# Where the scan of a state-space layer finds its input: PSUM bank or state tile

## The chip, the cores and the metric

The kernel runs on one core of a Trainium2 chip. The metric is the device time of one execution in microseconds. A core has five engines that work side by side, each with its own queue in order: PE (TensorE, matmuls), DVE (VectorE), ACT (ScalarE), POOL (GpSimd) and SP (SyncE, which here issues the DMAs). SBUF is the large on-chip memory, PSUM the small one that PE writes, in eight banks of 128 partitions by 512 floats. POOL works on SBUF only in this kernel.

## What is computed

Four images (4, 192, 56, 56) in float32 go through four layers: a local attention with an MLP, a frequency gating, an overlapping-window attention with a gated MLP, and a selective scan over the pixels in four directions. Only the last layer matters here. For each direction it computes, with 192 channels d and 4 states n per channel:

```python
def step(h, inp):
    dt_t, u_t, B_t, C_t = inp
    dA = jnp.exp(dt_t[..., None] * A)
    h = dA * h + dt_t[..., None] * B_t[:, :, None, :] * u_t[..., None]
    y = jnp.einsum('bkdn,bkn->bkd', h, C_t)
    return (h, y)
```

## The kernel before

The layer works in chunks of 448 pixels, seven to an image. A step `t` is one chunk of one image in one direction (4 images x 4 directions x 7 chunks = 112 steps). The 192 x 4 = 768 pairs of channel and state make six groups of 128 partitions; a half `h` (96 channels) is three of them. So there are 224 units `(t, h)` and 672 groups. For a unit, `scan(t, h)` does this:

- DVE multiplies `dt` by `u` into `du` (L2371 where the direction runs along rows, L2374 along columns, there with a strided `u`): 96 partitions, both inputs in SBUF.
- PE spreads each 32 channels of `du` over 128 partitions with a 0/1 matrix (L2381), into three PSUM banks.
- DVE multiplies each bank by B (`b_`, a tile in SBUF, called `bc` in the profile), in place in the bank (L2387). This is the product of dt u and B.
- DVE scans (L2403): `state = da * state + product` along the 448 pixels, `da` from SBUF, the product from the bank, the result into a state tile `st` in SBUF. The first value is a column of the state tile that the chunk before left.
- POOL multiplies the state tile by C (`c_`, also `bc` in the profile) into `da` (L2410): both inputs in SBUF.
- PE sums the four states of each channel (L2426), and DVE adds the sums into `y` (L2431, L2436 or L2440).

The decays `da` are made in `decay(t, h)`: a DMA spreads `dt` (L2348) and ACT takes the exponential (L2356). `load(t)` brings B, C and the low-rank dt from DRAM, `sizes` makes `dt` on PE (L2310) and ACT (L2322). Beside the scans run the front of the next image (`begin`: a layer norm L2079 to L2100, projections L2134, a depthwise convolution on PE L2167, ACT L2184, `product` L2218) and the end of the last one (`final`: a layer norm, a gate on POOL L2245, the output projection L2254, a sum on DVE L2265). Of the layer before, L1569 is a DVE multiply-add in its convolution, and L1430 a square on POOL.

The order of the instructions on every engine is fixed when the kernel is built. Each activity is a generator that yields, ahead of each piece of work, the engine, a cost, and the buffers that it takes; `Order.run` always starts the piece that can start first by these costs, with a small preference by place. `take` and `done` hand out and return buffers: `bank` is the pool of the eight PSUM banks, shared by everything that PE computes; `st` is 12 state tiles, `da` 10, `du` 3. A state tile is returned once the next chunk's scan has read its last column. The semaphores between the engines are put in by the tile framework from what is read and written.

Of the kernel before, what the change touches and what calls it, by code (L numbers as in the profile page):

```python
# [17 lines left out]
ALU = mybir.AluOpType  # L18
# [24 lines left out]
NS, DTR, SCH = 4, 12, 448  # L43
# [222 lines left out]
def rows2(ap, w=W):  # L266
    return ap.rearrange("p (y x) -> p y x", x=w)


class Order:  # L270
# [29 lines left out]
    def take(self, kind="bank"):  # L300
        slot = min((s for s in self.kinds[kind] if s[0] is not None), key=lambda s: s[0])
        slot[0] = None
        return slot[1]

    def done(self, tile):

        (slot,) = (s for slots in self.kinds.values() for s in slots if s[1] is tile)
        slot[0] = self.end + self.LATENCY
# [57 lines left out]
def on_pe(n, *takes, ready=None):  # L366

    return "PE", 0.0019 * n, takes, None, ready
# [6 lines left out]
def on_dve(*n, takes=(), ready=None, each=0.00105):  # L375
    return "DVE", sum(0.08 + each * i for i in n), takes, None, ready


def on_scan(n, ready):
    return "DVE", 0.1 + 0.0023 * n, ("st",), None, ready  # L380


def on_act(*n, takes=(), table=None, ready=None):
# [3 lines left out]
def on_pool(*n, each=0.0011, takes=()):  # L387
    return "POOL", sum(0.2 + each * i for i in n), takes, None, None
# [1601 lines left out]
def layer3(tc, order, pools, src, packs, aps, dst):  # L1990
# [7 lines left out]
    nc = tc.nc  # L1998
    take, done = order.take, order.done
# [71 lines left out]
    def gone(*what):  # L2071
        return what in passed
# [258 lines left out]
    def use(t, h):  # L2331

        users[t, h] = users.get((t, h), 0) + 1
        if users[t, h] == 2:
            done(sized[t][0][h])
# [23 lines left out]
    def scan(t, h):  # L2359

        b, o, s, c = steps[t]
        head = c == (NSC - 1 if s else 0)
        last = c == (0 if s else NSC - 1)
        px = slice(c * SCH, (c + 1) * SCH)
        yield lambda: t in sized and (2 * t + h == 0 or gone("multiplied", 2 * t + h - 1))
        dts, b_, c_ = sized[t]
        u = us[b % 2]
        yield on_dve(SCH, takes=("du",), each=0.0018 if o else 0.0015)
        du = take("du")
        if o == 0:  # L2370
            nc.vector.tensor_mul(du, dts[h], u[:HALF, h, px])  # L2371
        else:
            uv = u[:HALF, h].rearrange("p (y x) -> p x y", x=W)[:, 8 * c : 8 * c + 8]
            nc.vector.tensor_mul(rows2(du, H), rows2(dts[h], H), uv)  # L2374
        use(t, h)

        yield on_pe(500, *["bank"] * 3)
        tiles = [take() for _ in range(3)]
        for j in range(3):
            r = slice(32 * j, 32 * j + 32)  # L2380
            nc.tensor.matmul(tiles[j][:, :SCH], w["c96.rep"][r], du[r], start=True, stop=True)  # L2381
        done(du)
        passed.add(("multiplied", 2 * t + h))
        ends = []
        for j in range(3):
            yield on_dve(SCH, ready=order.end if j else None)
            nc.vector.tensor_mul(tiles[j][:, :SCH], tiles[j][:, :SCH], b_)  # L2387
            ends.append(order.end + order.LATENCY)
        if h == 1:
            done(b_)  # L2390
        das, sts = [], []
        for j in range(3):
            g = 3 * h + j
            yield lambda: (t, h, j) in decays and (head or (t - 1, g) in states)
            da, at = decays.pop((t, h, j))
            yield on_scan(SCH, ready=max(at, ends[j]))
            sts.append(take("st"))
            r = slice(None, None, -1 if s else 1)
            first = 0.0
            if not head:  # L2400
                before = states.pop((t - 1, g))
                first = before[:, 0:1] if s else before[:, SCH - 1 : SCH]
            nc.vector.tensor_tensor_scan(  # L2403
                sts[j][:, r], da[:, r], tiles[j][:, :SCH][:, r], first, ALU.mult, ALU.add
            )
            done(tiles[j])
            if not head:
                done(before)
            yield on_pool(SCH, each=0.0024)
            nc.gpsimd.tensor_mul(da, sts[j], c_)  # L2410
            das.append(da)
            if last:
                done(sts[j])
            else:
                states[t, g] = sts[j]
        if h == 1:
            done(c_)
            del sized[t]

        yield lambda: b == 0 or gone("read", b - 1, c if (o, s) == (0, 0) else 0)  # L2420
        yield lambda: (o, s) == (0, 0) or len(started) == 2 * NSC * (b + 1)
        yield lambda: s == 0 or o == 1 or added[b] >= 6 * NSC + 2 * (NSC - 1 - c) + h
        yield on_pe(600, "bank")
        py = take()
        for j in range(3):
            nc.tensor.matmul(py[32 * j : 32 * j + 32, :SCH], w["c128.sum"], das[j], start=True, stop=True)  # L2426
            done(das[j])
        yield on_dve(SCH)
        sums = py[:HALF, :SCH]
        if (o, s) == (0, 0):  # L2430
            nc.vector.scalar_tensor_tensor(  # L2431
                y[:HALF, h, px], u[:HALF, h, px], d_sum[:, h : h + 1], sums, ALU.mult, ALU.add
            )
            started.add((t, h))
        elif o == 0:
            nc.vector.tensor_add(y[:HALF, h, px], y[:HALF, h, px], sums)  # L2436
        else:

            yv = y[:HALF, h].rearrange("p (y x) -> p y x", x=W)[:, :, 8 * c : 8 * c + 8]
            nc.vector.tensor_add(yv, yv, sums.rearrange("p (x y) -> p y x", y=H))  # L2440
        done(py)
        added[b] += 1
        if o == 0 and s == 1 and h == 1:
            passed.add(("summed", b, c))
        if added[b] == 8 * NSC:
            passed.add(("scanned", b))
# [6 lines left out]
    n = 8 * NSC  # L2453
# [5 lines left out]
    for t in range(len(steps)):  # L2459
        add(2 * t - 5, load(t))  # L2460
        if t % 2 == 0:
            add(2 * t - 3, sizes((t, t + 1)))
        for h in range(2):
            add(2 * t + h - 1, decay(t, h))
            add(2 * t + h, scan(t, h))
# [5 lines left out]
    def keep_late(*args):  # L2471
        return keep(*args, pool=late)
# [7 lines left out]
        da=keep_late("da", [SCH], 10),  # L2480
        st=keep_late("st", [SCH], 12),
# [43 lines left out]
```

## Time and profile before

| | |
|---|---|
| median of 3 runs | 5724.87 us (5719.17 to 5725.76) |
| profiled execution | 5731.28 us, span 5729.5 us |
| mean granted TensorE clock | 0.929 |
| busy, whole span | PE 4866.4 us (85%), DVE 4140.6 (72%), ACT 2655.4 (46%), POOL 1699.9 (30%) |
| scans (L2403) | 672, from about 3990 to 5702 us |
| products (L2387) | 672, 415 us of DVE, 618 ns each |

In the lines of the profile an instruction is named by its line in the kernel, its engine, its operation and its tiles (`out<-in`), then shapes and count; a group's line ends with busy time, mean ns of one, and the engine's idle time before it with what ended it. `bank` is a PSUM bank; every other tile named here is in SBUF. In a timeline line the first number is the start and the second the time, in us. A line of one source line's instructions gives count, least, median and longest duration in ns, first and last start.

### The profile page before, as it was taken

Reading aid. Unit: us, or ns where it says so; the run is one execution under the profiler, and the core shown is the slowest. Engines: PE = TensorE matmul, PEld = TensorE weight load, DVE = VectorE, ACT = ScalarE, POOL = GpSimd, SP = SyncE. Lnnn points to the kernel's source line nnn. Section 1 sums busy time; section 2 is a strip of 40 time slices with the busy share of each in tenths; the row PEclk is TensorE's granted clock in tenths of the full one; section 3 lists DMA queues with packets and bytes.
Section 4 is the critical chain, followed back from the end, with each engine's and each line's share of the span. In section 5 each row is a group of like instructions: output and inputs, shape, how many; then the busy total and the mean of one; then the engine's idle time right before and its main releaser. Section 6 shows DMA issues by size and latency. Waiting matters only on the chain. (4 is left out here: it accounts for less than half of the span.)

```text
span 5729.5 us, 137267 instructions
## 1 busy us (share of the span) xinstructions
PE 4866.4 (85%) x58114; PEld 2407.0 (42%) x58114; DVE 4140.6 (72%) x6600; ACT 2655.4 (46%) x4271; POOL 1699.9 (30%) x1688
## 2 busy tenths in 40 slices
PE   4988998998899687898898888868888888888777
PEld 2444554454454444555555555534332232222112
DVE  5788447544744026888988888883678999998997
ACT  0122323212232215555555555546776776676544
POOL 0000000000000013433333433321345555555564
PEclk9999998999999798999999999989998999999998
DMA  6132224333332521000000000002456656566654
GB/s 185 53 80 60 66 60 105 64 88 91 76 69 56 99 77 37 14 22 21 17 22 18 19 20 21 16 26 60 122 135 157 160 145 172 155 149 167 165 149 109
DMA packets 356373, 475.97 MB, mean 83 GB/s; under 512 B 43600, under 2 KB 354256, under 8 KB 355248
## 3 DMA queue, kind: packets, MB, share of 16 engines
q1 hardware_dynamic: 355760, 467.20, 32.9%
q8 instruction: 458, 7.50, 0.5%
q14 instruction: 155, 1.27, 0.1%
HBM read 249.73 MB, written 63.17 MB: 55 GB/s over the span
## 5 line engine op out<-in xcount | busy, mean ns | idle before, releaser
L2410 POOL TENSOR_TENSOR da<-st,bc 128x448 f32<-128x448 f32 x672 | 857.0, 1281 | 751.5 <-DVE st L2403 600.1
L731 PE MATMUL bank<-X,wu 64*49 64x392 f32 x6720 | 610.5, 509 | 89.2 <-DVE X L710 85.9
L2403 DVE TENSOR_TENSOR_SCAN st<-da,st,bank 128x448 f32<-128x448 f32 x576 | 646.3, 1133 | 4.3 <-POOL da L2410 1.8
L838 POOL TENSOR_TENSOR attn<-attn,rs 112x1568 f32<-112x1568 f32 (+1 forms) x24 | 67.1, 2795 | 1726.5 <-DVE rs L836 989.9
L2356 ACT ACTIVATE da<-da,a_neg 128x448 f32<-128x448 f32 x672 | 410.1, 659 | 161.9 <-DMA da<-dt 150.2
L357 ACT ACT_TABLE_LOAD x373 | 478.6, 1283 | 6.6
L2387 DVE TENSOR_TENSOR bank<-bank,bc 128x448 f32<-128x448 f32 x672 | 382.9, 618 | 83.4 <-PE bank L2381 78.2
L731 PEld LDWEIGHTS bank<-X,wu 64*49 64x49 f32 x6720 | 247.6, 123 | 416.1 <-issue 366.4
L2426 PE MATMUL bank<-da,w_c 128*32 128x448 f32 x1344 | 348.8, 575 | 85.3 <-POOL da L2410 66.3
L2381 PE MATMUL bank<-du,w_c 32*128 32x448 f32 x1344 | 291.1, 643 | 105.2 <-DVE du L2371 59.2
L1569 DVE SCALAR_TENSOR_TENSOR bxn<-bapad,w_b,bxn 96x448 f32<-96x448 f32 (+2 forms) x448 | 318.7, 756 | 0.0
L1026 ACT ACTIVATE hm<-bank,w_a 128x448 f32<-128x448 f32 x168 | 106.3, 633 | 435.6 <-PE bank L1017 428.2
L1032 PE MATMUL bank<-hm,w_a 128*96 128x448 f32 x672 | 285.1, 555 | 16.7 <-ACT hm L1026 16.6
L1017 PE MATMUL bank<-xc,w_a 128*128 128x448 f32 x672 | 283.4, 551 | 0.6 <-DVE xc L998 0.6
L1430 POOL TENSOR_TENSOR bsq<-bsq 128x448 f32<-128x448 f32 (+7 forms) x120 | 144.5, 1206 | 446.9 <-ACT bsq L1427 401.8
L678 ACT ACTIVATE q<-bank,qk_bias,qk_scale 128x280 f32<-128x280 f32 (+2 forms) x216 | 116.9, 544 | 294.4 <-PE bank L664 251.2
L2134 PE MATMUL bank<-row,w_c 128*96 128x448 f32 x448 | 206.5, 599 | 29.7 <-DVE row L2100 27.9
L1488 PE MATMUL bank<-bxn,w_b 128*96 128x336 f32 (+2 forms) x576 | 214.3, 498 | 19.0 <-DVE bxn L1440 16.7
L754 ACT COPY sm<-bank 128x392 f32<-128x392 f32 x96 | 43.0, 489 | 380.6 <-PE bank L731 368.2
L2381 PEld LDWEIGHTS bank<-du,w_c 32*128 32x128 f32 x1344 | 92.1, 199 | 299.7 <-DVE du L2371 76.0
L998 DVE SCALAR_TENSOR_TENSOR xc<-bank,w_a,xc 96x224 f32<-96x224 f32 x112 | 44.9, 441 | 226.3 <-PE bank L988 124.5
L1763 PE MATMUL bank<-bzpad,b_diag 32*32 32x224 f32 (+2 forms) x8064 | 182.7, 371 | 24.1 <-ACT bzpad L1735 12.7
(333 smaller groups left out, 10015.4 us busy)
## 6 DMA issues: line engine op xcount, KB each, us to landing
da<-dt SPq DMA_DIRECT2D x672, 224.0 KB
vb<-vmem SPq DMA_DIRECT2D x576, 98.0 KB
bc<-prod SPq DMA_DIRECT2D x224, 224.0 KB
xq<-x SPq DMA_DIRECT2D x132, 210.0 KB
xc<-x SPq DMA_DIRECT2D x56, 336.0 KB
row<-x SPq DMA_DIRECT2D x56, 336.0 KB
xs<-x SPq DMA_DIRECT2D x28, 336.0 KB
vmem<-vt SPq DMA_DIRECT2D x56, 168.0 KB
```

What stands on the lines that cost most here:

```text
L357: self.nc.scalar.preload_act_table_set(table)
L731: nc.tensor.matmul(pm[a][outs[i], : WIN * W].rearrange("p (y x) -> p y x", x=W), wu[halves[a], k, dx], xt[halves[a], :, i, dx : dx + W], s ...
L1017: nc.tensor.matmul(ph[:, :CH], w["a128.c1T"][:, k, 128 * m : 128 * m + 128], xt[:, k], start=(k == 0), stop=(k == 1),)
L1032: nc.tensor.matmul(acc[h][:HALF, :CH], w["a128.c2T"][:, m, HALF * h : HALF * h + HALF], hm, start=(m == 0), stop=(m == 5),)
L1488: nc.tensor.matmul(rows2(pq[:HALF, :m]), w["b128." + wn][:, k, HALF * h : HALF * h + HALF], out[:, k], start=(k == 0), stop=(k == 1),)
L1569: nc.vector.scalar_tensor_tensor(dst, x, wt[:, t : t + 1], dst, ALU.mult, ALU.add)
L2356: nc.scalar.activation(da, da, AF.Exp, scale=a_neg[:, k, g : g + 1])
L2381: nc.tensor.matmul(tiles[j][:, :SCH], w["c96.rep"][r], du[r], start=True, stop=True)
L2387: nc.vector.tensor_mul(tiles[j][:, :SCH], tiles[j][:, :SCH], b_)
L2403: nc.vector.tensor_tensor_scan(sts[j][:, r], da[:, r], tiles[j][:, :SCH][:, r], first, ALU.mult, ALU.add)
L2410: nc.gpsimd.tensor_mul(da, sts[j], c_)
L2426: nc.tensor.matmul(py[32 * j : 32 * j + 32, :SCH], w["c128.sum"], das[j], start=True, stop=True)
```

## The change

The state tile is taken at the product instead of at the scan. The product writes it and returns the bank at once; the scan reads the product from the state tile and writes its result over it.

```diff
 def on_scan(n, ready):
-    return "DVE", 0.1 + 0.0023 * n, ("st",), None, ready
+    return "DVE", 0.1 + 0.0023 * n, (), None, ready
...
-        ends = []
+        ends, sts = [], []
         for j in range(3):
-            yield on_dve(SCH, ready=order.end if j else None)
-            nc.vector.tensor_mul(tiles[j][:, :SCH], tiles[j][:, :SCH], b_)
+            yield on_dve(SCH, takes=("st",), ready=order.end if j else None)
+            sts.append(take("st"))
+            nc.vector.tensor_mul(sts[j], tiles[j][:, :SCH], b_)
+            done(tiles[j])
             ends.append(order.end + order.LATENCY)
...
-        das, sts = [], []
+        das = []
...
             yield on_scan(SCH, ready=max(at, ends[j]))
-            sts.append(take("st"))
...
             nc.vector.tensor_tensor_scan(
-                sts[j][:, r], da[:, r], tiles[j][:, :SCH][:, r], first, ALU.mult, ALU.add
+                sts[j][:, r], da[:, r], sts[j][:, r], first, ALU.mult, ALU.add
             )
-            done(tiles[j])
```

Since the order on every engine is worked out from these costs and buffers, the order of the last layer's instructions can change with it.

## The prediction

> **What bounds the kernel now.** I read the page first: it gives one profiled execution of 5731.28 us (span 5729.5), 6.4 us above the median of 5724.87; the working below is made against 5731 and 6 us are taken off at the end. The change touches only the scans of the last layer, which run from 3980 to 5705 us, so the second view is the busy time by stretch, for the middle of that stage:
>
> ```profile
> core 0: us, PE busy (x) PEld busy (x) DVE busy (x) ACT busy (x) POOL busy (x), PEclk, DMA share, GB/s
> 4300.00:5650.00 1350.00, 1106.23 (x6709) 336.56 (x6710) 1237.75 (x1603) 872.92 (x1342) 764.33 (x610) 0.92 0.61 157
> ```
>
> DVE is busy 92% there (1237.75 of 1350) and idle for 112 us; over the whole stage (the same view for 3980 to 5705) it is busy 1507.69 of 1725, idle 217. POOL is busy 57%. So DVE sets the pace: time added to its queue moves the end, unless it fills one of these 217 us. Third, the page's groups:
>
> ```profile
> L2410 POOL TENSOR_TENSOR da<-st,bc 128x448 f32<-128x448 f32 x672 | 857.0, 1281 | 751.5 <-DVE st L2403 600.1
> L2403 DVE TENSOR_TENSOR_SCAN st<-da,st,bank 128x448 f32<-128x448 f32 x576 | 646.3, 1133 | 4.3 <-POOL da L2410 1.8
> L2387 DVE TENSOR_TENSOR bank<-bank,bc 128x448 f32<-128x448 f32 x672 | 382.9, 618 | 83.4 <-PE bank L2381 78.2
> ```
>
> Each scan (L2403) is followed by a POOL multiplication of its result (L2410). Fourth, what single lines took, least, median and most:
>
> ```profile
> L2371 DVE TENSOR_TENSOR du<-dt,u x112: 590/596/2593, 3980.6 to 5685.8; 96x448 f32<-96x448 f32 x112
> L2374 DVE TENSOR_TENSOR du<-dt,u x112: 946/970/1012, 4134.5 to 5574.9; 96x448 f32<-96x448 f32 x112
> L2440 DVE TENSOR_TENSOR y<-y,bank x112: 581/607/631, 4152.8 to 5589.6; 96x448 f32<-96x448 f32 x112
> L2403 DVE TENSOR_TENSOR_SCAN st<-da,st,bank x576: 1108/1135/1156, 4010.9 to 5700.4; 128x448 f32<-128x448 f32 x192
> L2410 POOL TENSOR_TENSOR da<-st,bc x672: 1119/1134/1852, 3990.8 to 5702.5; 128x448 f32<-128x448 f32 x168
> ```
>
> L2440 and L2403, with one large input in SBUF and one in PSUM, never stretch. L2371, with both large inputs in SBUF, stretches from 596 to 2593 ns, and POOL's L2410 from 1134 to 1852. The timeline shows why, at two places:
>
> ```profile
> 4356.17 1.13 POOL L2410 TENSOR_TENSOR da<-st,bc 128x448 f32<-128x448 f32 x1 [3.79 <-DVE st L2403]
> 4356.46 1.32 DVE L2371 TENSOR_TENSOR du<-dt,u 96x448 f32<-96x448 f32 x1
> ...
> 4621.39 0.97 DVE L2374 TENSOR_TENSOR du<-dt,u 96x448 f32<-96x448 f32 x1
> 4621.62 1.75 POOL L2410 TENSOR_TENSOR da<-st,bc 128x448 f32<-128x448 f32 x1 [1.50 <-DVE st L2403]
> 4622.27 1.15 DVE L2403 TENSOR_TENSOR_SCAN st<-da,st,bank 128x448 f32<-128x448 f32 x1
> ```
>
> At 4356 POOL is first (ends 4357.30); du, begun at 4356.46, ends 0.48 after that, at 4357.78. At 4621 du is first (ends 4622.36); POOL, begun inside it, ends 1.01 after that. The two exclude each other, whole instruction against whole instruction. The scan at 4622.27 lies over the same POOL instruction and takes its usual 1.15: today's scan is outside the exclusion. Its state column from SBUF (the first value) does not count; only its second large input in PSUM keeps it out. In the timeline 467 of the 672 scans lie beside POOL multiplications that read SBUF, 361 us in all.
>
> **The change, part by part.** (1) The product L2387 writes SBUF instead of PSUM. Nearest row: L2440, SBUF and PSUM in, SBUF out, 607 against 618 ns: -11 ns. It still reads one large input from SBUF, so like L2440 it stays out of the exclusion. (2) The scan reads its second input from SBUF: 607 against 596 (L2440 against L2371 undisturbed), again -11 ns. In place costs nothing: L2387 runs in place today. 672 x 22 ns = -15 us; bounds 0 and 672 x 2 x (618 - 594) = -32.
>
> (3) Banks come free one scan earlier. In the waits of the stage, PE waits for scans through banks 107 us in all (the largest: the weight loads of L2381 30.9, of L2310 25.0), but DVE feels PE only where it waits itself: 78.2 us for L2381, and those matmuls wait mostly for du. Bounds 0 and -78; I take -20. The Trainium skill, PSUM — Partial Sum Buffer, in its rules for kernel authors, advises to empty PSUM promptly because it is tight, which speaks for the change; had it the whole 107 us, the sum below would fall by another 87, to some +77.
>
> (4) A state tile is taken at the product, not at the scan. There are 12, 6 carry the last chunk's states, so 6 products may run ahead of their scans, two units of three; today three of 8 banks are held per unit, so at most two as well. The tile to be written was read by a POOL multiplication a chunk of work ago. I take 0 of a new wait, with the du and sums queued behind it as what it would hold up if the cover were gone.
>
> (5) The scan now has two large inputs in SBUF, da and st. No scan in this trace has that; the rows that do (L2371, L2374, and L1569 in the layer before) are all excluded with POOL, so I take it that the scan will be too; bounds: not at all, or always. The Trainium skill, SBUF — State Buffer, Who interferes with whom, says so for any DVE instruction with two SBUF inputs against a GpSimd instruction that reads SBUF, and speaks against this change; by the one row that is a scan, today's, the term below would be 0.
>
> Prices of (5). POOL behind DVE ends 0.99 after it (L2371: begins 0.16 into it, lasts 1.43, and 0.16 + 1.43 - 0.60). DVE behind POOL ends 0.115 sooner than it would alone from POOL's end (596 - 481), so a scan of 1.12 ends 1.00 after POOL. When both queue, they alternate: at 2427 two L1569 (0.67 alone) and two POOL multiplications take 3.02 together. From DVE's order in the timeline, with v the time from one excluded instruction's end to the next one's start (an overlap of 0.08 when adjacent):
> - du, then a scan at once: 117 times. POOL's multiplication of the scan before du goes in between: 0.88 + 0.08 = 0.96 late each (0.99 + 1.00 against v + 1.11); the sum over the true gaps is 110 us.
> - du, a sum into y (v 0.46), then a scan or du: 75 short covers of 0.40: 30 us.
> - scan, PSUM work, next scan: POOL starts 0.08 after the scan, so 1.10 - v. Three products (v 1.50, 107 times) cover it; one product or one sum (v 0.44) is short by 0.62, 103 times, 64 us; one layer-norm step or two products (v 0.9 to 1.0) 72 times by 0.2, 15 us.
> - scan, then a scan at once, 95 times: POOL's work is passed on, two multiplications under the next cover: between 0 and 0.96 each, half: 46 us.
>
> Sum 265 us. DVE's queue is in order, so behind a blocked scan stand the next products, du (which PE's L2381 waits for) and the sums into y. Part falls where DVE idles anyway, waiting for PE, which gets ahead: bounds none and all 217; I take a quarter of the waits, 66, since in the middle stretch only 8% is idle. So +265 - 66 - 15 - 20 = +164: 5895 in the profiled execution, 5889 as a median.
>
> **Rivals.**
> *POOL gives way.* POOL idles 803 us of the stage. Held claims after the change: scans 672 x 1.00, du 112 x (0.48 + 0.86), POOL 672 x 0.99 and its 28 longer ones (L2245) 28 x 1.93, together 1541 of 1725 us: they fit. Were the queue's order lucky, waits would fill idle time only: 265 - 217 - 15 = +33, 5758. Against it: the 117 and 103 places above recur in every chunk, and the order is fixed at build by costs that know of no exclusion (its chance covers an order that shifts for the better).
> *Faster.* The scan stays out of the exclusion, as its own row today has it. Then -15 and between 0 and -78 of (3), middle -39: -54, 5671. It decides from the scan's row alone: if the new scan beside POOL still takes 1.1 us at most, this holds. Against it: all three forms of DVE instruction with two large SBUF inputs in this trace exclude POOL.
> *Nothing.* Exclusion's cost beyond the idle time and gains cancel: within 11 us of 5725.
>
> **How the numbers follow.** My case 0.68: 5889; the sum's bounds are all of today's overlap, 361 - 15 = +346 (6071), and about +33. POOL gives way 0.18, all of it slower. Faster 0.10. Nothing 0.04. A change under 0.2% (11 us) can't be told from none here. Range 5750 to 6040: below it lie Faster and Nothing (0.14), above it some 0.05. Faster 0.10, same 0.04, slower 0.86.
>
> **What would show it.** L2403's median well above 1135 and its most near 2.1 to 3.2 us; L2410's median above 1134, up to 2.2; no scan over a POOL multiplication in the timeline; L2387 near 607; DVE's busy time in the stage up by 200 to 300 us and its idle time down; PE's waits for scans through banks gone from L2381 and L2310, the layers before unchanged. Wrong if L2403 stays at 1.1 us beside POOL, or if its waits are there and the stage is no longer.

## The result, and the profile after

The changed kernel takes 5976.36 us (median; 5972.85 to 5984.12) against 5724.06 us, a ratio of 1.0446 with a 95% interval of 1.0430 to 1.0461: 252 us slower. The forecast was 5889, slower, within 5750 to 6040. The profiled span is 5977.3 us, and the scan stage, from the first du to the last scan, is 1965.7 us against 1721.0 in the kernel before, which is the whole difference of the two spans but 3 us.

The same groups on the page of the changed kernel (the product is L2388 there, the scan L2404):

```profile
L2410 POOL TENSOR_TENSOR da<-st,bc 128x448 f32<-128x448 f32 x672 | 1162.4, 1746 | 655.8 <-DVE st L2404 575.0
L2404 DVE TENSOR_TENSOR_SCAN st<-da,st,st 128x448 f32<-128x448 f32 x576 | 804.2, 1407 | 3.0 <-ACT da L2356 2.7
L2388 DVE TENSOR_TENSOR st<-bank,bc 128x448 f32<-128x448 f32 x672 | 381.5, 608 | 85.2 <-PE bank L2381 60.1
```

The mean scan grew from 1133 to 1407 ns and POOL's multiplication from 1281 to 1746. The last columns, idle time before the instruction, don't hold this: the scans' is 3.0 us. The wait lies inside the instruction's own time. The least, median and most of single lines show it:

```profile
L2374 DVE TENSOR_TENSOR du<-dt,u x112: 953/973/1916, 4137.3 to 5801.6; 96x448 f32<-96x448 f32 x112
L2404 DVE TENSOR_TENSOR_SCAN st<-da,st,st x576: 1112/1143/3990, 4009.2 to 5946.3; 128x448 f32<-128x448 f32 x192
L2410 POOL TENSOR_TENSOR da<-st,bc x672: 1118/1804/5944, 3993.6 to 5951.5; 128x448 f32<-128x448 f32 x168
L2440 DVE TENSOR_TENSOR y<-y,bank x112: 581/609/619, 4162.7 to 5820.2; 96x448 f32<-96x448 f32 x112
```

The scan's least time is what it was (1112 ns against 1108), its median nearly so (1143 against 1135), its most is 3990 ns: 264 of the 672 scans take over 1250 ns, and they carry 183 of the 189 us that the scans grew by. L2440, with one input in PSUM, is still flat. The busy time by stretch, of the middle of the longer stage, shows where this ends:

```profile
core 0: us, PE busy (x) PEld busy (x) DVE busy (x) ACT busy (x) POOL busy (x), PEclk, DMA share, GB/s
4300.00:5900.00 1600.00, 1242.50 (x6994) 351.43 (x6990) 1445.54 (x1627) 895.17 (x1366) 1058.94 (x619) 0.86 0.53 135
```

DVE is 90% busy there (1445.54 of 1600), where it was 92%. Over the stage, from the same records: DVE busy 1724.9 us against 1507.1 (+218), idle 240.8 against 213.9 (+27). Of the +218, the scans make 944.7 - 755.8 = +189, du 227.1 - 203.4 = +24, the products -6; the remaining 11 are overlaps of neighbouring records, 145 us before and 133 now. PE's granted clock over the stage fell too, from 0.92 to 0.87; the experiments come back to it.

The timeline of the changed kernel has two forms of the turn-taking. DVE keeps it:

```profile
4106.85 5.31 DVE L2404 TENSOR_TENSOR_SCAN st<-da,st,st 128x448 f32<-128x448 f32 x5
4108.07 8.52 POOL L2410 TENSOR_TENSOR da<-st,bc 128x448 f32<-128x448 f32 x3 [9.22 <-DVE st L2404]
```

Five scans go through in 5.31 us. The POOL multiplication begun at 4108.07, inside the second of them, ends only 5.57 us later, after all of them. Or POOL keeps it:

```profile
4439.35 5.11 POOL L2245 TENSOR_TENSOR row<-row,gate 96x896 f32<-96x896 f32 x1 [10.97 <-DMA da<-dt]
4440.93 0.60 DVE L2371 TENSOR_TENSOR du<-dt,u 96x448 f32<-96x448 f32 x1
4441.45 5.05 DVE L2404 TENSOR_TENSOR_SCAN st<-da,st,st 128x448 f32<-128x448 f32 x2
4444.42 4.09 POOL L2410 TENSOR_TENSOR da<-st,bc 128x448 f32<-128x448 f32 x3
```

Here two scans take 5.05 us: the second, begun at 4442.51, stands behind POOL's gate (L2245, ends 4444.46) and one multiplication (ends 4445.56) and lasts 3.99.

### The profile page after: what moved, and what is told of

Same layout as the page of the kernel before. It is cut to its first block, busy times and chain, and to the rows that moved or that the text cites. A ratio compares the mean times of both kernels' runs of the same rounds, so it can differ in the third digit from the quotient of the medians.

```text
span 5977.3 us, 137326 instructions
## 1 busy us (share of the span) xinstructions
PE 4978.6 (83%) x58114; PEld 2402.0 (40%) x58114; DVE 4359.2 (73%) x6600; ACT 2651.5 (44%) x4267; POOL 2048.8 (34%) x1688
## 5 line engine op out<-in xcount | busy, mean ns | idle before, releaser
L2410 POOL TENSOR_TENSOR da<-st,bc 128x448 f32<-128x448 f32 x672 | 1162.4, 1746 | 655.8 <-DVE st L2404 575.0
L2404 DVE TENSOR_TENSOR_SCAN st<-da,st,st 128x448 f32<-128x448 f32 x576 | 804.2, 1407 | 3.0 <-ACT da L2356 2.7
L2426 PE MATMUL bank<-da,w_c 128*32 128x448 f32 x1344 | 471.3, 620 | 218.1 <-POOL da L2410 201.8
L2388 DVE TENSOR_TENSOR st<-bank,bc 128x448 f32<-128x448 f32 x672 | 381.5, 608 | 85.2 <-PE bank L2381 60.1
L2381 PE MATMUL bank<-du,w_c 32*128 32x448 f32 x1344 | 272.5, 661 | 95.2 <-DVE du L2371 55.5
L2426 PEld LDWEIGHTS bank<-da,w_c 128*32 128x32 f32 x1344 | 68.6, 114 | 584.1 <-POOL da L2410 483.1
L2322 ACT ACTIVATE dt<-bank,w_c 96x448 f32<-96x448 f32 x224 | 129.1, 624 | 229.7 <-PE bank L2310 125.8
```

Of the source, the lines that this page charges most:

```text
L2388: nc.vector.tensor_mul(sts[j], tiles[j][:, :SCH], b_)
L2404: nc.vector.tensor_tensor_scan(sts[j][:, r], da[:, r], sts[j][:, r], first, ALU.mult, ALU.add)
```

## The experiments

The theory: the scan, now with two large inputs in SBUF, and POOL's multiplication, which reads SBUF, exclude each other, and DVE's queue pays. The rivals: the order of the queues, which the planner (`Order.run`) worked out anew because banks and state tiles are taken and returned elsewhere (all five queues differ); and the scan itself, slower in place or from SBUF. "Before" and "after" in the names of the runs are the two kernels that they start from.

**Only the scan's input, in the old order.** PE's, ACT's and POOL's queues are row for row those of the kernel before.

```diff
-                sts[j][:, r], da[:, r], tiles[j][:, :SCH][:, r], first, ALU.mult, ALU.add
+                sts[j][:, r], da[:, r], c_[:, r], first, ALU.mult, ALU.add
```

> The kernel before with one operand changed: the scan's second input is the C tile in SBUF instead of the product in its bank (the product is still computed and is left out of the scan). The order on every queue stays that of the kernel before. If exclusion between the scan and POOL's multiplication is the cost: scans stretched by 190 to 300 us in all, the time up by 180 to 300 us (1.03 to 1.052). If the changed order of the queues is the cost: within 0.3% of before, scans at 1.13 us. If reading SBUF makes the scan itself slower: scans longer also where POOL is idle.

Measured 1.0472 (1.0445 to 1.0498): the whole loss, without any change of order and without scanning in place. Its multiplications and scans:

```profile
L2410 POOL TENSOR_TENSOR da<-st,bc x672: 1118/1834/4407, 3983.6 to 5944.6; 128x448 f32<-128x448 f32 x168
L2403 DVE TENSOR_TENSOR_SCAN st<-da,st,bc x576: 1112/1145/3987, 4001.3 to 5939.5; 128x448 f32<-128x448 f32 x192
```

The most is 3987 ns; the 123 scans with no POOL multiplication beside them average 1133, so reading SBUF doesn't make the scan itself slower. The scans grew by 182 us in all, a little under the 190 expected at least.

**The change in the old order.** `done(tiles[j])`, which tells the planner that the bank is free, goes from the product to after the scan; PE's and ACT's queues are again those of before.

```diff
             nc.vector.tensor_mul(sts[j], tiles[j][:, :SCH], b_)
-            done(tiles[j])
...
                 sts[j][:, r], da[:, r], sts[j][:, r], first, ALU.mult, ALU.add
             )
+            done(tiles[j])
```

> The kernel after, but the product's bank is kept until after the scan, as before; PE's and ACT's queues then have the order of the kernel before. Exclusion as the cost: 1.035 to 1.05, the difference to the changed kernel (1.0446) being what the earlier release of the bank and the order that follows from it are worth (20 us of gain expected, so bank_held 20 us slower than the changed kernel). The changed order as the cost: below 1.015.

Measured 1.0468 (1.0446 to 1.0490). The changed kernel's 1.0446 lies 13 us lower, but the intervals overlap: from the two, the new order is worth between nothing and an estimated 28 us. The run holds the bank in the plan only. On the chip the semaphores follow what is read and written, and the scan doesn't read the bank: PE's weight loads of L2381 waited for scans for 10.3 us here, 13.8 in the changed kernel and 30.9 before. So the release itself is in this run too, and no run tests it alone.

**Exclusion taken away, in both kernels.** POOL writes the same tile and reads nothing:

```diff
-            nc.gpsimd.tensor_mul(da, sts[j], c_)
+            nc.gpsimd.memset(da, 0.0)
+            nc.gpsimd.memset(da, 0.0)
```

> The kernel before with POOL's multiplication of the state by C replaced by two memsets of the same tile, which write SBUF and read none (the product with C is left out). Exclusion needs a POOL instruction that reads SBUF: du no longer stretches (596 and 970 ns flat), POOL's memsets don't either; 0 to 60 us faster than before. If any POOL work excludes: du still stretches to over 1 us in places.

> The changed kernel with the same replacement. Exclusion as the cost: within 40 us of memset_before, rather 15 to 35 us faster than it, scans at 1.13 us. The changed order or a slower scan as the cost: 150 to 250 us slower than memset_before, as the changed kernel is against the kernel before.

Measured 1.0007 (0.9996 to 1.0018) and 1.0006 (0.9996 to 1.0016): the loss of the changed kernel is gone to within 0.1%, with all the rest of the change in place. In its timeline:

```profile
4599.78 3.24 DVE L2404 TENSOR_TENSOR_SCAN st<-da,st,st 128x448 f32<-128x448 f32 x3
4600.99 0.47 POOL L2410 MEMSET da<- 128x448 f32 x1 [4.13 <-DVE st L2404]
4601.52 0.47 POOL L2411 MEMSET da<- 128x448 f32 x1
4602.04 0.47 POOL L2410 MEMSET da<- 128x448 f32 x1
```

Three scans take 3.24 us, 1.08 each, with POOL at work from 4600.99 on: a POOL instruction that only writes doesn't hold DVE up. (Two memsets, 1.00 us from the first's start to the second's end, stand for a multiplication of 1.13.) Two things were not as expected. Du still stretched in places (to 1.6 us in memset_before and 2.4 in memset_after) and so did 16 scans of memset_after (21 us in all); all of those scans lie beside POOL instructions that read, the gate L2245 or a copy. And memset_before is not faster than before, though du takes 17 us less: the time did not follow so small a wait.

**Doses.** The change for some of a unit's three groups only, shown for the first group, against the kernel before:

```diff
-            yield on_dve(SCH, ready=order.end if j else None)
-            nc.vector.tensor_mul(tiles[j][:, :SCH], tiles[j][:, :SCH], b_)
+            yield on_dve(SCH, takes=() if j else ("st",), ready=order.end if j else None)
+            if j == 0:
+                sts[0] = take("st")
+                nc.vector.tensor_mul(sts[0], tiles[0][:, :SCH], b_)
+                done(tiles[0])
+            else:
+                nc.vector.tensor_mul(tiles[j][:, :SCH], tiles[j][:, :SCH], b_)
...
-                sts[j][:, r], da[:, r], tiles[j][:, :SCH][:, r], first, ALU.mult, ALU.add
+                sts[j][:, r], da[:, r], (tiles[j][:, :SCH] if j else sts[0])[:, r], first, ALU.mult, ALU.add
```

> The change made for the first of a unit's three groups only (224 of the 672 scans read the product from the state tile). If each such scan costs its share of what the three cost: waits of some 70 us in scans and du, the time up by 50 to 110 us (1.009 to 1.019). If POOL can give way as long as the claims are few: below 1.005.

> The change made for the third of a unit's three groups only. In the trace of the kernel before, the scans of the first, second and third group lie beside POOL multiplications for 46, 152 and 163 us. If a scan's cost goes by what it lay beside (213 us of stretch for 361 us in the changed kernel, 0.59 each): 96 us, 1.012 to 1.021, three times the first group's 1.0054. If only the number of such scans counts: again 1.004 to 1.007.

> The change made for the second and third group. By what they lay beside, 315 us x 0.59 = 186 us: 1.027 to 1.037. By number alone: twice the first group's, 1.009 to 1.013. If what counts is that POOL's backlog runs from group to group, less than the sum of the parts: near last_group.

| groups | ratio (interval) | scans + us | DVE busy + us | DVE idle + us |
|---|---|---|---|---|
| first | 1.0054 (1.0037 to 1.0071) | 17 | 28 | 2 |
| third | 1.0071 (1.0056 to 1.0086) | 57 | 64 | -32 |
| second, third | 1.0225 (1.0208 to 1.0242) | 142 | 154 | -30 |
| all | 1.0446 (1.0430 to 1.0461) | 189 | 218 | 27 |

All three measured ratios lie below what I expected from the share. The stretch goes by place: the third group's scans lose over three times what the first's do (57 against 17 us), as the 163 against 46 us beside POOL in the old trace said (3.5 times). But the rate doesn't hold: scans and du together lost 0.57 of that overlap for the first group, 0.38 for the third, 0.49 for second and third and 0.59 for all. The third group's time alone would also fit "by number"; the 1.0225 of second and third does not. The time follows DVE's busy time and its idle time: idle time swallowed some 30 us in two of the four, nothing in the first, and grew in the last. The parts also don't add up: the third group's scans lose 57 us alone, 86 with the second changed and 99 with all, the first's 17 alone and 31 with all. I read that as POOL's backlog running from group to group, which these numbers allow but don't show by themselves.

**A planner that knows of a late POOL.** In the changed kernel, only the cost is altered:

```diff
-            yield on_pool(SCH, each=0.0024)
+            yield on_pool(SCH, each=0.0045)
             nc.gpsimd.tensor_mul(da, sts[j], c_)
```

> The changed kernel, built with 2.2 instead of 1.28 us as POOL's cost of the multiplication by C, so that the order puts the sums into y later. If DVE's idle time before these sums (105 us after, 62 before) is the order's blindness for a late POOL: it falls by 30 to 60 us and the time to 1.034 to 1.041. If the time is only that DVE and POOL take turns: the waits in the scans stay and the time is within 15 us of the changed kernel's (1.042 to 1.047).

Measured 1.0381 (1.0364 to 1.0398), 36 us below the changed kernel. The waits of the changed kernel that this aimed at are these (who waits, for whom, us in total, times, longest):

```profile
PEld bank L2426 <- POOL da L2410: 483.1, 329, 5.7
DVE y L2431 <- PE bank L2426: 41.1, 19, 12.9
DVE y L2440 <- PE bank L2426: 39.0, 34, 4.0
DVE y L2436 <- PE bank L2426: 24.9, 18, 6.2
```

The first of them in the kernel before:

```profile
PEld bank L2426 <- POOL da L2410: 243.1, 233, 3.7
```

The sums' weight loads wait for POOL (243 us before, 483 after), and DVE for the sums (60 us before, 105 after). With the new order the first falls to 259 us, DVE's idle before the sums by 27 us, a little less than expected, its idle in all by 24 and its busy time by 14; the scans' stretch falls only from 189 to 175. So most of the idle time that grew is the late POOL, handed on through PE, as far as one new order of all queues can show it. A lower clock of PE doesn't explain it: over the stage it was 0.85 here, below the changed kernel's 0.87, and 0.89 in du_pool_before, the fastest kernel of all, against 0.92 before.

**Du on POOL.** The experiments say that DVE and POOL should not both have instructions with two SBUF inputs that meet. In the kernel before, du was the only such instruction on DVE in the stage; here POOL computes it.

```diff
-        yield on_dve(SCH, takes=("du",), each=0.0018 if o else 0.0015)
+        yield on_pool(SCH, takes=("du",), each=0.0024)
...
-            nc.vector.tensor_mul(du, dts[h], u[:HALF, h, px])
+            nc.gpsimd.tensor_mul(du, dts[h], u[:HALF, h, px])
...
-            nc.vector.tensor_mul(rows2(du, H), rows2(dts[h], H), uv)
+            nc.gpsimd.tensor_mul(rows2(du, H), rows2(dts[h], H), uv)
```

> The kernel before with du computed on POOL instead of DVE: DVE loses its 203 us of du and with it every instruction of the scan stage with two large SBUF inputs; POOL gains 224 multiplications, 270 to 360 us, so some 72% of the stage. If DVE's queue sets the pace: 80 to 200 us faster (0.965 to 0.986), POOL's L2410 flat at 1.13 us. If the loop over POOL and PE sets it: within 1% of before, DVE's idle time up by what du took.

> The changed kernel with du on POOL. Exclusion of the scans alone, against a POOL that is busier by a quarter: slower than du_pool_before by 150 to 350 us. If du's exclusion was a large part of the loss: slower than du_pool_before by less than 120 us.

Measured 0.9808 (0.9792 to 0.9824), 5615.75 us, faster than both kernels; and 1.0315 (1.0299 to 1.0330) with the change in. The pair differs by 288 us, 36 us more than the change cost without it; POOL, busier by du, has more instructions to exclude a scan with, and the scans grew by 313 us instead of 189. In the first of the two, the lines of POOL:

```profile
L2410 POOL TENSOR_TENSOR da<-st,bc x672: 1122/1135/1155, 3987.7 to 5576.4; 128x448 f32<-128x448 f32 x168
L2371 POOL TENSOR_TENSOR du<-dt,u x112: 1122/1133/1152, 3977.6 to 5556.0; 96x448 f32<-96x448 f32 x112
L2374 POOL TENSOR_TENSOR du<-dt,u x112: 1341/1358/1392, 4122.1 to 5460.8; 96x448 f32<-96x448 f32 x112
```

All are flat now. DVE is busy for 1322 us where it was for 1507, and only 106 of these 185 us came off the time. Most of the 185 is work that left DVE: of du's 203 us only some 28 were stretch (L2371 alone takes 596 ns and averaged 845). So this run doesn't say that moving an instruction with two SBUF inputs pays more than moving another.

## Why the prediction was right, and where it was not

**The mechanism** was right: point (5), taken from du's rows, holds for the scan, which no row had shown. scan_reads_c and the memset pair show it from both sides: the input alone brings the whole loss, and without POOL's multiplications that read the loss is gone. The statement of the Trainium skill (SBUF — State Buffer, Who interferes with whom) covered the scan too, and the memsets agree with its restriction to GpSimd instructions that read. Of the rivals, Faster fell with the scan's row, Nothing with the time, and POOL gives way with the dose of all three; something like it is seen at the small doses (1.0054, 1.0071). The prediction counted three forms of DVE instruction with two large SBUF inputs; the trace has more, which point the same way: L1917 takes 948 ns in the median and up to 1807 in the layer before.

**Its signs** came true in part: DVE's busy time rose by 218 us and L2388 fell to 608 ns. But the scan's median stayed at 1143 ns, since most scans don't wait at all, its most was 3990 and not 3200, POOL's went to 5.9 us and not 2.2, the records of waiting scans do lie over POOL's, idle time rose instead of falling, and PE's waits for scans through banks fell without going away.

**The wait term** was too large: 265 us against 213 measured in the scans and du. The step that failed is "When both queue, they alternate". I had it from one place in the layer before. In the changed kernel's timeline, of 229 places where two excluded DVE instructions stand side by side and a POOL one is already waiting, DVE kept its turn at 114 and POOL came between at 115. For du followed by a scan, priced at 110 us, POOL came between at 51 of 107 places, for 45 us. On the other side, a scan followed by du, which I had priced at nothing, waited at 43 places for 42 us, since a POOL instruction was already waiting there. So the term came as near as it did because these two misses offset each other. (In its sum, 103 places at 1.10 - 0.44 would be 68 us and not 64.)

**The absorbed share** had the wrong sign: I let idle time swallow 66 us; it grew by 27. The step that failed is that PE "gets ahead" while DVE waits. PE's sums hang on POOL, POOL was late by the same exclusion, and DVE then waited for the sums, 105 us instead of 60 (pool_cost_after). Where the third group, or the second and third, were changed, idle time did swallow 30 us. This term was the larger miss, 93 us, and the wait term's 52 us the other way hid part of it, which was luck.

**The small terms.** The product fell from 618 to 608 ns, as its row said. The scan did not get shorter: with no POOL instruction beside it, 1142 ns in memset_after against 1137 from PSUM in memset_before, where I had -11. The earlier bank, taken at -20 us, can't be told from nothing: the memset pair differs by 0.01%, though memset_after's scans and du hold 23 us more than memset_before's, behind which a gain of that size could hide; against bank_held it is the order only, 0 to 28 us. The advice of the Trainium skill (PSUM — Partial Sum Buffer, Summary: rules for kernel authors) to empty PSUM promptly brought no gain that these runs can tell from none: PE's waits for scans through banks fell (the weight loads of L2381 waited 30.9 us before, 13.8 after) and the time did not.

So +164 came out of +265 - 66 - 15 - 20, and +252 out of +218 and +27 in the stage, with some 7 us of run-to-run and outside it.

**Open:** what decides who gets the next turn when both wait. No run was made for it; neither the kind of the two DVE instructions nor a semaphore wait on the second separates the 114 from the 115.

## What to carry to other kernels

Before an operand is moved from PSUM to SBUF to free a bank, count the large SBUF inputs of the instruction that reads it: a DVE instruction that goes from one to two starts to take turns with POOL instructions that read SBUF (here multiplications, a gate and a copy), and its waits show only as longer instructions. The time that the two lie side by side in the old trace warns of the price but doesn't give it: here between 0.38 and 0.59 of it became waits. POOL's lateness comes back through whoever waits for POOL. If POOL has room, moving a DVE instruction with two SBUF inputs to it can pay; here it took 1.9% off the kernel before.

## What the runs showed of the hardware

- Neither engine is served in order of arrival: four scans of 1.12 us ended while one POOL multiplication waited, which then ended 5.57 us after its start instead of 1.13; and a scan waited 2.9 us for the rest of one POOL instruction and the whole of a second, which began after it.
- POOL memsets of 128x448 (0.47 us) beside scans with two SBUF inputs stretch neither.
- A scan over 448 elements that starts from a column of the tile before costs the same from PSUM and from SBUF, within 1%: 1137 ns from PSUM (memset_before), 1142 from SBUF in place (memset_after) and 1140 from SBUF not in place (scan_reads_c), each with no POOL instruction beside it.
